# A graph layer's last 70 microseconds: output inside the condition, last squares on TensorE, residual loaded early

## The chip, the cores and the metric

The kernel runs on one core of one Trainium2 chip. Its time is device time in microseconds, the median of several executions. A core has a matrix engine (TensorE, PE in the profile, with its weight loads as PEld), three engines for elementwise work (VectorE or DVE, ScalarE or ACT, GpSimd or POOL) and a queue for transfers (SyncE, SP). Each engine works through its own list of instructions in order, and waits on semaphores for the others.

## The reference

One message-passing layer over 12,500 nodes and 412,500 edges, 96 features, float32. Edges are sorted by destination.

```
def _mlp(h, W, b, gamma, beta):
    h = relu(h @ W + b)
    mu, var = mean(h, axis=0), mean((h - mu)**2, axis=0)
    return gamma * (h - mu) * rsqrt(var + EPS) + beta

node_feat = _mlp(x, W_node, ...)
edge_feat = _mlp(edge_attr, W_edge, ...)
message   = _mlp(concat([x[src], x[dst], edge_feat]), W_msg, ...)
out       = layernorm(x + segment_sum(message, dst) + node_feat)
```

The normalization inside `_mlp` is over all rows, so the messages' statistics (the mean and the mean square of each of the 96 features over all edges) are complete only when the last edge has been worked on, and the output can start only then.

## The kernel before, in words

**Stages.** First the node tables `p_tab` and `q_tab` are computed (node features times two parts of `W_msg`) and written to memory; then the node part is computed, and x plus the node part, centred, is written to memory as `y0_d` (L257 to L287); then the edge part's statistics (L289 to L341); then comes the message loop (L379 to L630); then a condition (L785, L786); then the output (L790 to L827).

**Groups and blocks.** An edge tile has 128 edges. Four tiles are a group of 512 edges (806 groups), four groups are a block (202 blocks). For each tile GpSimd issues one indirect DMA (`gather`, L171) that fetches 128 rows of `p_tab`. GpSimd's whole list is these gathers, 3223 of them. The first 26 blocks are gathered before the loop and written to `spill` through two `stage` buffers; they are read back as `pb`. All other groups go into a ring of 26 buffers (`ring`, L93, tiles named `pg`). Each time the loop has used a group of the ring, the gather of the group 26 further on is issued (L619).

**The loop.** The order is written by hand (L566): for the loop, SP, GpSimd, TensorE, VectorE and ScalarE run their instructions in the order in which the program text issues them. For step `k`, `linear` (L475) computes the rest of the message on TensorE into `z`; `message` (L483) adds the gathered rows on VectorE and once a block builds `at`, a matrix of zeros and ones that says which edge belongs to which node; `first_part`, `second_part` and `third_part` (L502 to L530) apply the relu and split the result into three bf16 parts `h`; ScalarE also squares it into `sq`; `sums` (L532) multiplies `at` with `h` on TensorE, which sums the messages by node; `fold`, `turn` and `add` (L546 to L563) put the block's sums into `agg`, transposed by TensorE (`turn`), and the row of ones' sum into `total`. `moments` (L511) reduces `sq` over the tiles on VectorE and adds it to `squares`; after the loop one product with a column of ones sums `squares` over the partitions (L625). The last block has two groups, the last of them three tiles, so the last two steps are done singly.

**The condition.** The loop works only if every block's destinations lie within a window of nodes; `flag` says whether one does not. After the loop every engine loads the flag into a register (L785) and compares (L786). If the flag is set, `general` computes the same sums in another way, with long loops. With these inputs it isn't set, and each engine jumps over that code.

**The output.** Four products into an unused tile `busy` come first (L794). `norm` (L138) turns the statistics into a factor and an offset per feature; they are multiplied into a centring matrix `d` (L800, L802). Then come 13 groups of eight node blocks (the last has two): TensorE multiplies eight blocks of `agg` with `d` into `py` (three buffers), VectorE adds the residual `y0`, ScalarE squares, VectorE reduces over the features, ScalarE takes the root, VectorE the reciprocal, GpSimd multiplies, and SP's queue writes 384 KB out. The residual is loaded by ScalarE's queue into six buffers. Here the scheduler orders the instructions by itself.

Of the kernel before, what the change touches and what calls it, by code (L numbers as in the profile page):

```python
# [11 lines left out]
F32 = mybir.dt.float32  # L12
# [11 lines left out]
P = 128  # L24
# [17 lines left out]
NBK = 4  # L42
# [18 lines left out]
BUSY = 4  # L61
# [15 lines left out]
def gnn(ctx, tc, t):  # L77
# [13 lines left out]
    rpool, xpool = ExitStack(), ExitStack()  # L91
    nc.sync.dma_start(src_raw, t["src"][:, :RAW * BG * GT])
    ring = rpool.enter_context(tc.tile_pool(name="ring", bufs=RING))  # L93
# [86 lines left out]
    def blocks():  # L180

        for b in range(SPILL // BG):
            pg = ring.tile([P, BG, GT, C], F32, name="stage", bufs=2)
# [159 lines left out]
    def fast(ring):  # L343
        def ahead_of(g):
            return gather(g, ring.tile([P, GT, C], F32, name="pg"))

        with tc.manual_schedule(engines={ET.SP, ET.Pool}):
            nc.sync.dma_start(q_tab[:WM, :], zero[:WM])
            for r in range(WM + NN, WT, 64):
                n = min(64, WT - r)  # L350
                nc.sync.dma_start(q_tab[r:r + n, :], zero[:n])
            next(store)
            places()
            next(store)
            next(store)
            for i, _ in enumerate(nodes()):
                if i in (1, 5, 10):
                    next(store)
            xpool.close()
            n = 0  # L360
            for i, _ in enumerate(edge_norm()):
                if 73 * i >= 50 + 100 * n:
                    next(store, None)
                    n += 1
            for _ in store:
                pass
            got = {g: ahead_of(g) for g in range(SPILL, SPILL + RING)}
# [11 lines left out]
        with tc.tile_pool(name="fix", bufs=1) as fix, tc.tile_pool(name="msg", bufs=2) as work, \  # L379
# [63 lines left out]

            def convert(s):

                b = order[s]
                px = ps.tile([P, 2, GE], F32, name="pr", bufs=1)
                for i in range(BG):
                    for k in range(GT):
                        nc.tensor.transpose(px[:C, 0, k * P:(k + 1) * P], got[b * BG + i][:, k, :], ident)  # L450
                    xt = work.tile([C, GE], F32, name="xt", bufs=1)
                    nc.scalar.activation(xt, px[:C, 0, :], AF.Copy)
                    for k in range(GT):
                        nc.tensor.matmul(px[:, 1, k * C:(k + 1) * C], xt[:, k * P:(k + 1) * P], w_msg[:, 0, :],
                                         start=True, stop=True)
                    nc.vector.tensor_copy(got[b * BG + i], px[:, 1, :GT * C].rearrange("p (k c) -> p k c", c=C))
# [26 lines left out]
            def message(k):  # L483
# [5 lines left out]
                if i == min(2, NG - 1 - (g - i)):  # L489
# [64 lines left out]
            def add(s):  # L554

# [3 lines left out]
                    skip_runtime_bounds_check_because="they are nodes' numbers")  # L559
                pt = pas.pop(s)[:C + 1, GE - P:GE - P + NW]  # L560
                to = agg[:, bass.ds(val[0], NW - 1)]
                nc.vector.tensor_tensor(to, pt[:, :NW - 1], to, op=OP.add)
                nc.vector.tensor_add(total, pt[:, NW - 1:], total)  # L563

            n, ahead = len(steps), SPILL + RING
            with tc.manual_schedule(engines={ET.SP, ET.Pool, ET.PE, ET.DVE, ET.Activation}):  # L566
                load(0)
# [10 lines left out]
                for k in range(len(order) * BG + LATER + BG):  # L578
                    s, g = steps[min(k, n - 1)]
                    if k < n and g % BG == 0:  # L580
# [3 lines left out]
                    if k < n:  # L584
                        message(k)
                    j = k - LATER - BG - 1
                    if k < n and (k % 2 or k >= last):
                        whole, m = k < last, min(GT, NT - g * GT)
                        part = (k - 1,) if whole else (k, 1, m)
                        now = first_part(*part)  # L590
                        if waiting:
                            moments(*waiting)
                        waiting = now if whole else None
                        second_part(*part)
                    if j >= 0 and j % BG == 0:
                        fold(j // BG)
                    if j >= 2 and j % BG == 2:
                        add(j // BG)
                    if k < n and (k % 2 or k >= last):
                        third_part(*part)  # L600
                        if not whole:
                            moments(*now, min(P, E - (g * GT + m - 1) * P))
                    if j >= 1 and j % BG == 1:
                        turn(j // BG)
                    if 0 <= k - LATER < n:
                        sums(k - LATER)
                    if k < n and g % BG != 3 and s + 1 < len(order):
# [4 lines left out]
                    if k < n and g % BG == 3:  # L612
# [6 lines left out]
                    if k < n and g >= SPILL and ahead < NG:  # L619
# [4 lines left out]
            pq = ps.tile([P, GE], F32, name="pa")  # L624
            nc.tensor.matmul(pq[:C, :1], squares, ones, start=True, stop=True)  # L625
            nc.vector.tensor_scalar(s[:, 0:1], pq[:C, :1], 1.0 / E, None, op0=OP.mult)
# [3 lines left out]
            nc.vector.tensor_scalar(mstat[:, 1:2], s[:, 2:3], 0.0, None, op0=OP.max)  # L630

    def general():

        with tc.tile_pool(name="gd", bufs=1, space=DRAM) as gd, tc.tile_pool(name="gfix", bufs=1) as fix, \
# [31 lines left out]
            def gather(idx_s, idx_d, c, nt, rows):  # L666
                pg = work.tile([P, GT, C], F32, name="pg", bufs=4)
                qg = work.tile([P, GT, C], F32, name="qg", bufs=4)
# [7 lines left out]
            def message(n, gathered, ea, dstf, to_spare, c, nt, rows, stat):  # L676
# [13 lines left out]
                same = work.tile([P, GT, P], F32, name="same", bufs=3)  # L690
# [25 lines left out]
                sums = work.tile([P, GT, W], F32, name="sums", bufs=3)  # L716
# [25 lines left out]
            AHEAD = 2  # L742
            with tc.For_i(0, NI, 1) as it:
# [3 lines left out]
                for g in range(-AHEAD, IG):  # L747
# [4 lines left out]
                    ea = work.tile([EK, GE], F32, name="gea", bufs=3)  # L752
# [9 lines left out]
            for j, (t0, nt, rows) in enumerate(REST):  # L762
# [4 lines left out]
                ea = work.tile([EK, GE], F32, name="gea", bufs=3)  # L767
# [15 lines left out]
    fast(ring)  # L783
    rpool.close()
    bad = nc.values_load(flag, min_val=0, max_val=1, skip_runtime_bounds_check_because="a comparison's result")  # L785
    with tc.If(bad):  # L786
        general()


    with tc.tile_pool(name="fin", bufs=2) as work, tc.tile_pool(name="fin_ps", bufs=2, space=PSUM) as ps:  # L790

        busy = ps.tile([P, GE], F32, name="busy", bufs=1)
        for i in range(BUSY):
            nc.tensor.matmul(busy, ident, rel[:, i * P:(i + 1) * P, :].rearrange("p g t -> p (g t)"), start=True, stop=True)  # L794
        a_m, c_m = norm(mstat, v["g_msg"], v["beta_msg"], "msg")
        l = const.tile([C, C + 1], F32, name="l")
        nc.vector.tensor_scalar(l[:, :C], ident[:C, :C], a_m, None, op0=OP.mult)
        nc.vector.tensor_copy(l[:, C:C + 1], c_m)
        pd = ps.tile([C + 1, C], F32, name="pd", bufs=1)
        nc.tensor.matmul(pd, l, center, start=True, stop=True)  # L800
        d = const.tile([C + 1, C], F32, name="dm")
        nc.vector.tensor_copy(d, pd)  # L802

        out = t["out"]
        for i in range(0, NB, NBY):
            n = min(NBY, NB - i)
            y0 = work.tile([P, NBY, C], F32, name="y0", bufs=6)
            nc.scalar.dma_start(y0[:, :n, :], y0_d[i // NBY][:, :n * C].rearrange("p (b f) -> p b f", f=C))
            py = ps.tile([P, 2, GE], F32, name="py", bufs=3)
            for g in range(n):  # L810
                nc.tensor.matmul(py[:, g // NBK, g % NBK * C:(g % NBK + 1) * C],  # L811
                                 agg[:, WM + (i + g) * P:WM + (i + g + 1) * P], d, start=True, stop=True)
            sq = work.tile([P, NBY, C], F32, name="sq")
            sd = work.tile([P, NBY], F32, name="sd", bufs=3)
            y = work.tile([P, NBY, C], F32, name="y", bufs=3)
            if n == NBY:
                x = y0.rearrange("p (k b) f -> p k (b f)", k=2)
                nc.vector.tensor_add(x, py[:, :, :NBK * C], x)  # L818
            else:
                x = y0[:, :n, :].rearrange("p b f -> p (b f)")  # L820
                nc.vector.tensor_add(x, py[:, 0, :n * C], x)
            nc.scalar.activation(sq[:, :n, :], y0[:, :n, :], AF.Square)
            nc.vector.tensor_reduce(sd[:, :n], sq[:, :n, :], axis=AX.X, op=OP.add)  # L823
            nc.scalar.activation(sd[:, :n], sd[:, :n], AF.Sqrt, bias=eps, scale=1.0 / C)  # L824
            nc.vector.reciprocal(sd[:, :n], sd[:, :n])  # L825
            nc.gpsimd.tensor_tensor(y[:, :n, :], y0[:, :n, :], sd[:, :n].unsqueeze(2).to_broadcast([P, n, C]), op=OP.mult)  # L826
            nc.sync.dma_start(out.rearrange("(b p) f -> p b f", p=P)[:, i:i + n, :], y[:, :n, :])  # L827
# [34 lines left out]
```

## Time and profile before

| | us |
|---|---|
| median of 3 runs | 4117.61 (4116.02 to 4118.02) |
| the profiled execution | 4122.05 |
| its span, first to last instruction | 4120.3 |

| engine | busy us | share |
|---|---|---|
| TensorE, products | 3150.0 | 76% |
| TensorE, weight loads | 2259.1 | 55% |
| VectorE | 2576.7 | 63% |
| ScalarE | 2020.8 | 49% |
| GpSimd | 3067.8 | 74% |

Mean granted TensorE clock: 0.629 of full speed.

A row of the timeline reads: start, length, engine, line, operation, what it writes and reads, the number of instructions merged into the row, and in brackets the idle time of the engine before it with what ended it. A row of the stretches reads: from and to, its length, busy time of the engine asked for with the number of its instructions, the granted clock, the share of the DMA engines that was busy, and GB/s. Products in f32 appear as two records each. Starts of neighbouring instructions on one engine can overlap a little.

### The profile page before, as it was taken

The numbers are of one execution on the slowest core, as the hardware profiler recorded it, in microseconds if no ns is written. First come the engines' busy times: TensorE is split into PE (matmuls) and PEld (weight loads), VectorE is DVE, ScalarE is ACT, GpSimd is POOL, SyncE is SP. The second block draws the span as 40 slices with busy tenths as digits, with TensorE's granted clock in tenths as the row PEclk, the third lists the DMA queues.
The fourth block names the chain that finished last, engine by engine and source line by source line (L and its number), as shares of the span: only waits on it lengthen the run. The fifth ranks groups of instructions, "written<-read, shape, count | busy, mean of one in ns | idle before, by whom it ended". The sixth has DMA issues, their size and how long they took to land. (4 is left out here: it accounts for less than half of the span.)

```text
span 4120.3 us, 42684 instructions
## 1 busy us (share of the span) xinstructions
PE 3150.0 (76%) x13498; PEld 2259.1 (55%) x13498; DVE 2576.7 (63%) x4038; ACT 2020.8 (49%) x2418; POOL 3067.8 (74%) x3244
## 2 busy tenths in 40 slices
PE   4699967888878777777777677877777777777776
PEld 4465535666655555555555555555555555555554
DVE  2599994667766655665566556655666566655665
ACT  1287754556644444544444444544454454444443
POOL 6777777777777777777777777777777777777774
PEclk7655556667665656666666666666666666656666
DMA  8555532222222222222222222222222222222224
GB/s 244 168 117 107 106 78 57 54 54 56 56 54 46 54 52 55 52 48 53 53 48 53 53 55 53 46 54 54 54 46 54 53 54 46 54 53 55 46 53 112
DMA packets 190368, 274.07 MB, mean 67 GB/s; under 512 B 121571, under 2 KB 121956, under 8 KB 189126
## 3 DMA queue, kind: packets, MB, share of 16 engines
q0 software_dynamic: 103136, 158.62, 19.4%
q1 hardware_dynamic: 71684, 99.14, 8.7%
q10 hardware_dynamic: 15312, 13.47, 1.2%
q8 instruction: 111, 1.82, 0.2%
q14 instruction: 125, 1.02, 0.1%
HBM read 227.55 MB, written 43.43 MB: 66 GB/s over the span
## 5 line engine op out<-in xcount | busy, mean ns | idle before, releaser
L175 POOL DMA_INDIRECT pg<-p_tab,src x2807 | 2649.5, 944 | 856.1 <-issue 692.1
L479 PEld LDWEIGHTS z<-rhs,left 128*128 128x128 f32 x6446 | 1291.4, 295 | 1033.1 <-DVE h L530 909.0
L479 PE MATMUL z<-rhs,left 128*128 128x96 f32 x6446 | 1381.7, 386 | 588.5 <-DVE h L530 587.0
L542 PE MATMUL pa<-h,at 128*80 128x291 bf16 x3223 | 837.8, 406 | 191.1 <-DVE at L492 185.0
L505 ACT ACTIVATE h<-z 128x768 bf16<-128x768 f32 x404 | 330.1, 817 | 1324.0 <-DVE z L488 1315.9
L488 DVE TENSOR_TENSOR z<-z,pg 128x384 f32<-128x384 f32 x702 | 395.0, 563 | 783.1 <-DMA pg<-p_tab,src 771.5
L542 PEld LDWEIGHTS <-at 128*80 128x80 bf16 x3223 | 496.1, 167 | 300.9 <-DVE at L492 228.4
L515 DVE TENSOR_REDUCE sum_of<-sq 128x96 f32<-128x768 f32 x404 | 591.9, 1465 | 0.0
L473 ACT ACTIVATE left<-pr 127x1024 f32<-127x1024 f32 x403 | 411.0, 1020 | 347.5 <-PE pr L465 346.9
L530 DVE TENSOR_TENSOR h<-z,h 128x768 bf16<-128x768 f32 x404 | 387.0, 958 | 244.2 <-ACT h L525 244.1
L465 PE MATMUL pr<-ea,we 7*127 7x512 f32 x1404 | 512.3, 813 | 17.3 <-DMA ea<-rel_d 12.5
L175 POOL DMA_INDIRECT stage<-p_tab,src x368 | 353.9, 962 | 128.3 <-issue 106.8
L524 DVE SCALAR_TENSOR_TENSOR z<-z,h 128x768 f32<-128x768 f32 x404 | 387.3, 959 | 28.2 <-ACT sq L507 28.1
L306 PE MATMUL pr<-ea,wide 10*128 10x512 f32 x1212 | 371.3, 1061 | 21.2 <-DMA ea<-in_ea 21.2
L312 DVE BATCH_NORM_STATS2 estats<-r 128x6 f32<-128x512 f32 x606 | 361.2, 676 | 27.6 <-ACT r L310 27.6
L310 ACT ACTIVATE r<-pr 128x1024 f32<-128x1024 f32 x303 | 292.9, 1024 | 143.6 <-PE pr L306 116.9
L525 ACT ACTIVATE h<-z 128x768 bf16<-128x768 f32 x404 | 329.2, 815 | 66.7 <-DVE z L524 66.7
L508 ACT ACTIVATE sq<-sq 128x768 f32<-128x768 f32 x404 | 339.7, 841 | 13.1
L507 ACT ACTIVATE sq<-z 128x768 f32<-128x768 f32 x404 | 322.9, 799 | 0.0
L306 PEld LDWEIGHTS pr<-ea,wide 10*128 10x128 f32 x1212 | 208.2, 319 | 182.9 <-issue 81.0
L492 DVE TENSOR_TENSOR at<-rel,z 128x496 bf16<-128x496 f32 x202 | 135.6, 671 | 262.3 <-PE z L479 262.0
L465 PEld LDWEIGHTS pr<-ea,we 7*127 7x127 f32 x1404 | 135.0, 236 | 139.4 <-issue 108.6
(127 smaller groups left out, 1145.2 us busy)
## 6 DMA issues: line engine op xcount, KB each, us to landing
pg<-p_tab,src POOLq DMA_INDIRECT x2807
spill<-stage SPq DMA_DIRECT2D x26, 768.0 KB
pb<-spill SPq DMA_DIRECT2D x26, 768.0 KB
ea<-in_ea SPq DMA_DIRECT2D x75, 160.0 KB
rhs<-q_tab SPq DMA_DIRECT2D x202, 46.5 KB
ea<-in_ea SPq DMA_DIRECT2D x352, 20.0 KB
stage<-p_tab,src POOLq DMA_INDIRECT x368
y_d<-y0s SPq DMA_DIRECT2D x12, 384.0 KB
```

What stands on the lines that cost most here:

```text
L175: nc.gpsimd.indirect_dma_start(out=pg[:, i, :], out_offset=None, in_=tab[:, :], in_offset=bass.IndirectOffsetOnAxis(ap=idx[:, k:k + 1], ax ...
L306: nc.tensor.matmul(pr[:, k % 2, :], wide[Q * i:Q * i + 2 * EK, :], ea[Q * i:Q * i + 2 * EK, b % J, :], start=True, stop=True)
L312: nc.vector.bn_stats(stats[:, (k - o) % NS, (k - o) // NS, :], r[:, 1 - o, :])
L465: nc.tensor.matmul(prs[s, half][:C + WN, i, :], we[o:o + EK + 2, :], block[s][o:o + EK + 2, :], start=True, stop=True)
L473: nc.scalar.activation(x[:C + WN, 2 * half:2 * half + n, :], pr[:C + WN, :n, :], AF.Relu)
L479: nc.tensor.matmul(zb[k // 2 % 2][:, k % 2, i * C:(i + 1) * C], left[s % 2][:KR, g % BG, i * P:(i + 1) * P], rhs[:KR, s % RB, g % BG, :], ...
L488: nc.vector.tensor_add(z, z, got.pop(g)[:, :n, :])
L508: nc.scalar.activation(sq[:, :m, :n, :], sq[:, :m, :n, :], AF.Square)
L515: nc.vector.tensor_reduce(sum_of, sq[:, :m, :whole, :].rearrange("p g t c -> p c g t"), axis=AX.XY, op=OP.add)
L524: nc.vector.scalar_tensor_tensor(z, z, 0.0, h[0], op0=OP.max, op1=OP.subtract)
L530: nc.vector.tensor_tensor(h[2], z, h[1], op=OP.subtract)
L542: nc.tensor.matmul(pas[s][:NW, :3 * (C + 1)], at[s % HB][:r, i, o + NW * t:o + NW * (t + 1)], h[:r, t, :, :].rearrange("p a c -> p (a c)") ...
```

## The change

- **Ring and stage.** The ring has 13 buffers of two groups for 26 of one. The `stage` buffers have a pool of their own, closed before the loop.
- **Residual.** Where the ring has no further group to gather, the pairs that come free take the 13 pieces of `y0_d`, loaded by SP's queue, each when both groups of the pair have been used.
- **The flag** is loaded into registers ahead of the loop, on every engine, so on GpSimd between two gathers.
- **The last two steps** are written out. The last `moments` of VectorE are gone: `columns` multiplies each tile's squares with a column of ones on TensorE and accumulates in PSUM (one product for `squares`, 8, 4, 2 and 1 for the last tiles). `at` of the last block is built one group earlier. `add` takes `total` first.
- **The output** is a function that stands in both arms of the condition; the arm that these inputs take follows the comparison directly, and it ends with a jump over the other arm. The `busy` products are gone. In the last but one group ScalarE scales, in eight instructions, and in the last VectorE; GpSimd does the other eleven.
- In the arm that is not taken, `general` has fewer buffers.

```diff
-    ring = rpool.enter_context(tc.tile_pool(name="ring", bufs=RING))
+    ring = rpool.enter_context(tc.tile_pool(name="ring", bufs=RING // 2))
+    stage = spool.enter_context(tc.tile_pool(name="stage", bufs=2))
...
     def fast(ring):
+        y0s, pair = [], [None]
+
         def ahead_of(g):
-            return gather(g, ring.tile([P, GT, C], F32, name="pg"))
+            if g % 2 == 0:
+                pair[0] = ring.tile([P, 2, GT, C], F32, name="pg")
+            if g < NG:
+                return gather(g, pair[0][:, g % 2, :, :])
+            i = (g - NG) // 2
+            if g % 2 == 0 and i * NBY < NB:
+                y0s.append(pair[0].rearrange("p g t c -> p (g t c)"))
+                m = min(NBY, NB - i * NBY) * C
+                nc.sync.dma_start(y0s[i][:, :m], y0_d[i][:, :m])
...
+            def columns(to, x):
+                for i in range(x.shape[1]):
+                    nc.tensor.matmul(to, x[:, i, :], ones, start=False, stop=False)
...
-                if i == min(2, NG - 1 - (g - i)):
+                if i == (2 if g - i + BG <= NG else 0):
...
+                nc.vector.tensor_add(total, pt[:, NW - 1:], total)
                 nc.vector.tensor_tensor(to, pt[:, :NW - 1], to, op=OP.add)
-                nc.vector.tensor_add(total, pt[:, NW - 1:], total)
...
             with tc.manual_schedule(engines={ET.SP, ET.Pool, ET.PE, ET.DVE, ET.Activation}):
+                bad = nc.values_load(flag, min_val=0, max_val=1, skip_runtime_bounds_check_because="a comparison's result")
...
+                s, g = len(order) - 1, steps[last][1]
+                m, r = NT - (g + 1) * GT, E - (NT - 1) * P
+                message(last)
+                sq = first_part(last, 1, GT)[0]
+                turn(s - 2)
+                sums(last - 2)
+                sums(last - 1)
+                square_sum = ps.tile([P, 2, GE], F32, name="pr", bufs=1)[:C, 0, :1]
+                nc.tensor.matmul(square_sum, squares, ones, start=True, stop=False)
+                for i in range(2):
+                    columns(square_sum, waiting[0][:, i, :, :])
+                add(s - 2, place(s - 2))
+                second_part(last, 1, GT)
+                third_part(last, 1, GT)
+                ahead_of(ahead)
+                message(n - 1)
+                sq_end = first_part(n - 1, 1, m)[0]
+                fold(s - 1)
+                turn(s - 1)
+                sums(last)
+                columns(square_sum, sq[:, 0, :, :])
+                second_part(n - 1, 1, m)
+                third_part(n - 1, 1, m)
+                sums(n - 1)
+                columns(square_sum, sq_end[:, 0, :m - 1, :])
+                nc.tensor.matmul(square_sum, sq_end[:r, 0, m - 1, :], ones[:r], start=False, stop=True)
+                add(s - 1, place(s - 1))
+                at_end = place(s)
+                fold(s)
+                turn(s)
+                add(s, at_end)
+                ahead_of(ahead + 1)
...
+    y0s, bad = fast(ring)
+    with tc.If(bad, preferred_fallthrough_block=False) as cmp:
+        general()
+        output(y0s, "gen")
+    with cmp.Else():
+        output(y0s, "win")
     rpool.close()
-    bad = nc.values_load(flag, min_val=0, max_val=1, skip_runtime_bounds_check_because="a comparison's result")
-    with tc.If(bad):
-        general()
...
-        busy = ps.tile([P, GE], F32, name="busy", bufs=1)
-        for i in range(BUSY):
-            nc.tensor.matmul(busy, ident, rel[:, i * P:(i + 1) * P, :].rearrange("p g t -> p (g t)"), start=True, stop=True)
...
-            y0 = work.tile([P, NBY, C], F32, name="y0", bufs=6)
-            nc.scalar.dma_start(y0[:, :n, :], y0_d[i // NBY][:, :n * C].rearrange("p (b f) -> p b f", f=C))
...
-            nc.gpsimd.tensor_tensor(y[:, :n, :], y0[:, :n, :], sd[:, :n].unsqueeze(2).to_broadcast([P, n, C]), op=OP.mult)
...
+                if i == last - 1:
+                    for g in range(n):
+                        nc.scalar.activation(y[:, g, :], y[:, g, :], AF.Copy, scale=sd[:, g:g + 1])
+                else:
+                    (nc.vector if i == last else nc.gpsimd).tensor_tensor(y[:, :n, :], y[:, :n, :], by, op=OP.mult)
```

More of the change, by code (lines that the diff above doesn't have):

```diff
@@ L60 @@
 CL, CE = 2, 2
-BUSY = 4
 J = 8
@@ L182, in blocks @@
         for b in range(SPILL // BG):
-            pg = ring.tile([P, BG, GT, C], F32, name="stage", bufs=2)
+            pg = stage.tile([P, BG, GT, C], F32, name="stage")
             for i in range(BG):
@@ L577, in fast @@
                 waiting, last = None, BG * (len(order) - 1)
-                for k in range(len(order) * BG + LATER + BG):
-                    s, g = steps[min(k, n - 1)]
-                    if k < n and g % BG == 0:
+                for k in range(last):
+                    s, g = steps[k]
+                    if g % BG == 0:
                         if s + 2 < len(order):
@@ L583, in fast @@
                             fetch(s + 2)
-                    if k < n:
-                        message(k)
+                    message(k)
                     j = k - LATER - BG - 1
[L587 to L590, printed above, removed]
+                    if k % 2:
+                        now = first_part(k - 1)
                         if waiting:
                             moments(*waiting)
-                        waiting = now if whole else None
-                        second_part(*part)
+                        waiting = now
+                        second_part(k - 1)
                     if j >= 0 and j % BG == 0:
@@ L597, in fast @@
                     if j >= 2 and j % BG == 2:
[L598 to L602, printed above, removed]
+                        add(j // BG, place(j // BG))
+                    if k % 2:
+                        third_part(k - 1)
                     if j >= 1 and j % BG == 1:
                         turn(j // BG)
-                    if 0 <= k - LATER < n:
+                    if k >= LATER:
                         sums(k - LATER)
-                    if k < n and g % BG != 3 and s + 1 < len(order):
+                    if g % BG != 3 and s + 1 < len(order):
                         if g % 2:
@@ L618, in fast @@
                         linear(k + 3)
[L619 removed]
+                    if g >= SPILL:
                         got[ahead] = ahead_of(ahead)
                         ahead += 1
+                s, g = len(order) - 1, steps[last][1]
[30 more added lines that the diff above has]
+                ahead_of(ahead + 1)
             s = fix.tile([C, 3], F32, name="s")
[L624 to L626 removed]
+            nc.vector.tensor_scalar(s[:, 0:1], square_sum, 1.0 / E, None, op0=OP.mult)
             nc.vector.tensor_scalar(mstat[:, 0:1], total[:C], 1.0 / E, None, op0=OP.mult)
@@ L689, in message @@
                                         ident[:rows, :rows])
-                same = work.tile([P, GT, P], F32, name="same", bufs=3)
+                same = work.tile([P, GT, P], F32, name="same", bufs=2)
                 nc.vector.tensor_tensor(
```

86 lines of the change are left out of this document (45 added, 41 removed).

## The prediction

> **What bounds the kernel now.** I read the page's groups first, then GpSimd's waits, then the timeline of the last 70 us, then the stretches with their granted clock.
>
> ```profile
> span 4120.3 us, 42684 instructions
> ...
> L175 POOL DMA_INDIRECT pg<-p_tab,src x2807 | 2649.5, 944 | 856.1 <-issue 692.1
> ```
> ```profile
> POOL pg L175 <- issue: 692.1, 2271, 0.3
> ...
> POOL pg L175 <- DMA pg<-p_tab,src: 69.2, 225, 0.9
> ...
> POOL pg L175 <- DVE total L563: 26.5, 87, 0.3
> ```
>
> A gather takes 0.94 us and is followed by 0.30 us of idle, whatever the releaser named: the longest idle time behind VectorE is 0.3 us. So GpSimd issues one gather each 1.25 us without a stop from the first `pg` to the last, and the ring is never full. All that is added on GpSimd's queue counts in full; what the other engines do before the last gather counts for nothing. The rest of the time is the tail:
>
> ```profile
> 4051.64 0.94 POOL L175 DMA_INDIRECT pg<-p_tab,src  x1 [0.30 <-issue]
> ...
> 4055.80 0.57 DVE L488 TENSOR_TENSOR z<-z,pg 128x384 f32<-128x384 f32 x1 [3.67 <-DMA pg<-p_tab,src]
> ...
> 4060.40 0.94 POOL L175 DMA_INDIRECT pg<-p_tab,src  x1 [0.30 <-issue]
> 4060.73 0.56 DVE L488 TENSOR_TENSOR z<-z,pg 128x384 f32<-128x384 f32 x1
> 4060.87 2.11 PE L542 MATMUL pa<-h,at 128*80 128x291 bf16 x8 [1.03 <-DVE h L530]
> ...
> 4065.47 0.46 DVE L488 TENSOR_TENSOR z<-z,pg 128x288 f32<-128x288 f32 x1
> 4065.96 0.42 DVE L492 TENSOR_TENSOR at<-rel,z 128x248 bf16<-128x248 f32 x1
> ...
> 4068.02 1.93 PE L542 MATMUL pa<-h,at 128*80 128x291 bf16 x7 [5.05 <-DVE total L563]
> 4068.10 0.46 DVE L530 TENSOR_TENSOR h<-z,h 128x288 bf16<-128x288 f32 x1
> ...
> 4071.08 0.43 PE L552 MATMUL pa<-ident,by_node 80*97 80x80 f32 x1
> ...
> 4072.45 0.15 DVE L630 TENSOR_SCALAR mstat<-s 96x1 f32<-96x1 f32 x1
> 4075.75 0.29 ACT L141 ACTIVATE norm_msg<-mstat,eps 96x1 f32<-96x1 f32 x1 [7.68 <-DVEq L786]
> ...
> 4075.86 6.24 PE L794 MATMUL busy<-rel,ident 128*128 128x512 f32 x8 [4.35 <-DVEq L786]
> ...
> 4076.90 0.15 DVE L798 COPY l<-norm_msg 96x1 f32<-96x1 f32 x1
> ...
> 4082.31 0.26 DVE L802 COPY dm<-pd 97x96 f32<-97x96 f32 x1 [5.26 <-PE pd L800]
> 4082.62 21.63 PEld L811 LDWEIGHTS py<-dm,agg 97*128 97x128 f32 x192 [0.51 <-DVE dm L802]
> 4082.62 21.79 PE L811 MATMUL py<-dm,agg 97*128 97x96 f32 x192 [0.35 <-DVE dm L802]
> 4084.74 0.96 DVE L818 TENSOR_TENSOR y<-py,y 128x768 f32<-128x768 f32 x1 [2.17 <-DMA y<-y_d]
> ...
> 4113.06 0.17 DVE L825 RECIPROCAL sd<-sd 128x2 f32<-128x2 f32 x1 [0.36 <-ACT sd L824]
> 4113.81 2.06 POOL L826 TENSOR_TENSOR y<-y,sd 128x768 f32<-128x768 f32 x2 [0.20 <-POOL y L826]
> ```
>
> Read: a gather lands 4.16 us after it starts (4051.64 to 4055.80). The statistics stand at 4072.60; all engines pass the condition's load and jump, and ScalarE starts the norm 3.15 us later; `l` is ready at 4077.05, but TensorE works on the eight `busy` records until 4082.10; the output products start at 4082.62 and the output takes 37.7 us from there.
>
> **The clock.** This decides the case.
>
> ```profile
> 166.08 28.48 PE L278 MATMUL py<-center,xp 96*128 96x96 f32 x132 [7.74 <-DVE y0s L282]
> ```
> ```profile
> 166.00:168.00 2.00, 1.92 (x9) 0.50 0.57 206
> ...
> 192.00:194.00 2.00, 2.00 (x11) 0.50 0.99 392
> ```
> ```profile
> 4080.00:4081.00 1.00, 1.00 (x2) 0.50 0.86 252
> 4081.00:4082.00 1.00, 1.00 (x4) 0.98 0.90 249
> ...
> 4103.00:4104.00 1.00, 1.00 (x11) 1.00 1.16 327
> ```
>
> The column behind TensorE's busy time is the granted clock. The `busy` products (128 rows, 512 columns) raise it from 0.50 to 1.00 at 4081.0, 5.1 us after they start, and the output runs on at 1.00: 21.79 us for 192 records, 0.113 us each. The nodes' products of L278 have nearly the output's form (96 rows for 97, 96 columns moving, f32), ran without a pause for 28.48 us and stayed at 0.50 in every stretch: 0.214 to 0.216 us each. Without `busy`, the output starts at 0.50, and the nearest row says that it stays there.
>
> **Part by part.** (1) Ring of pairs, `stage` in its own pool: each second gather now waits for a group one later; with no idle time over 0.3 us behind VectorE that is nothing, and the cover is a ring of 26 groups (130 us of issue). (2) The flag is loaded before the loop, on GpSimd's queue as well, between two gathers. No row has that load. On VectorE the load of `base` lies hidden:
>
> ```profile
> 3966.49 0.96 DVE L524 SCALAR_TENSOR_TENSOR z<-z,h 128x768 f32<-128x768 f32 x1
> ...
> 3967.36 0.23 DVE L562 TENSOR_TENSOR agg<-pa,agg 97x79 f32 x1
> ```
>
> It takes at most 0.87 us of sequencer time; bounds 0 to 0.9, taken 0.6, since GpSimd shows no overlap between instructions. (3) Residual loads move from ScalarE's queue into the last 130 us on SP's, 13 of them, each waiting for the pair's last message; `load` of the next blocks stands behind on SP, but its rows are wanted a block (20 us) later. Against the gathers in flight they could cost the landing of the next to last group a microsecond or two, which (4) hides. In the output they take away the waits behind `y<-y_d`, the first 2.17 us.
>
> (4) Last squares on TensorE. VectorE loses reductions and adds between 4060.7 and 4069.4; the last message can start when its gather lands, 4060.40 + 4.16 = 4064.56 for 4065.47, and `at` is built a group earlier: its `h` is ready at 4064.56 + (4068.56 - 4065.47 - 0.42) = 4067.2. But TensorE gets 16 products of one column, two records each, in its strict order.
>
> ```profile
> 607.18 1.09 PE L330 MATMUL pr<-part,pick 128*96 128x2 f32 x6 [20.17 <-DVE part L319]
> ...
> 4009.87 1.86 PE L479 MATMUL z<-rhs,left 128*128 128x96 f32 x8
> ```
>
> Nearest is L330 (same weights, two columns, clock 0.50): six records with their end in 1.09 us, some 0.16 us each; the other end is the 0.232 us of a record with 96 columns. At 0.16: nine products end at 4062.98 + 2.8 = 4065.8, the turn and four sums take 1.2 (4067.0), four products 1.3 (4068.3), the last three sums 0.9 (4069.2), three products 1.0 (4070.2); the last turn, issued as the last of these drain, starts near 4069.8, and from its start to the statistics it is 1.5 us (4071.08 to 4072.60): they stand at some 4071.3, 1.3 us gained. At 0.232 it is 2.3 us later, a loss of 1.
>
> (5) Near arm: the norm starts 0.1 us behind the statistics for 3.15: 4071.4. `l` takes 1.30 us as before (4075.75 to 4077.05): 4072.7. The centring product and `dm` take 1.2 at half clock (0.5 between 4082.10 and 4082.62): 4073.9, with the flag's 0.6 4074.5. `busy` (L794) no longer holds TensorE. So the output starts 8.1 us earlier. The jump over the other arm now stands at the arm's end; its 2 to 3 us run beside the last transfer, and I add 0.3 (0 to 2.5).
>
> (6) Output. At 0.50: 196 records by 0.214 us are 41.9 us, for the 22 of before; TensorE then bounds the stage, since VectorE needs some 2 us for eight blocks (0.96 + 0.90 + 0.17) and TensorE 3.4.
>
> ```profile
> 4066.41 0.41 ACT L505 ACTIVATE h<-z 128x288 bf16<-128x288 f32 x1 [2.45 <-DVE at L492]
> 4066.72 0.40 ACT L507 ACTIVATE sq<-z 128x288 f32<-128x288 f32 x1
> ...
> 4105.29 0.90 DVE L823 TENSOR_REDUCE sd<-sq 128x8 f32<-128x768 f32 x1
> ...
> 4110.44 0.35 DVE L821 TENSOR_TENSOR y<-py,y 128x192 f32<-128x192 f32 x1
> ...
> 4110.87 0.36 ACT L822 ACTIVATE sq<-y 128x192 f32<-128x192 f32 x1
> ```
>
> Behind the last full products (41.3): add 0.96, square 0.84, reduction 0.90, root and reciprocal with the small group's add 0.6, eight scalings on ScalarE at about 0.22 each 1.9 (estimated from 0.41 us durations 0.31 apart for 288 columns), the small group's root, reciprocal and product 0.9: 47.4 us. From the last product to the end of the span stand 4120.3 - 4115.87 = 4.4 us, and the jump's 0.3: 52.1 us.
>
> **Sum.** 4074.5 + 52.1 = 4126.6 for a span of 4120.3, 6.3 us longer: 8.1 gained ahead of the output, 14.4 lost in it. The profiled execution took 4122.05 us with 1.75 around its span; the median of the three runs is 4117.61, 4.4 below. I carry the difference over: 4117.6 + 6.3 = 4123.9.
>
> **Rivals.** A: the output's products raise the clock themselves. For it: they have 97 rows, which may count otherwise than 96, and z products with sums do raise it within the loop; against it, L278. With the clock doubled 5 us in, the second group is ready at 6.2 us, VectorE's remaining work (11 full groups' adds, 12 reductions and reciprocals, the small add: 23.7 us at those durations) ends at 29.9, scalings and last group 3.0, the end 4.7: 37.6. 4074.5 + 37.6 = 4112.1, 8.2 less, and with the first groups a little earlier 9: 4108.6 to 4109.4, taken 4109. [...]
>
> B, slower: the one-column products go at the 96-column pace, so TensorE's tail is 2.3 us later: 4126.2. It decides from about 0.22 us a record, with the clock at 0.50. Against it: L330.
>
> C: the near arm is no near arm, that is, the condition still jumps for 3 us: 4127. Against it: in the program's list the arm's instructions follow the comparison directly.
>
> **How the numbers follow.** 0.2% (8.2 us) is about what a measurement of this kernel can tell: 4109.4 and 4125.8 are the bounds. Forecast 58%: 4123.9, own range 4120.5 (flag 0, pace of the columns faster, clock late) to 4126.5 (flag 0.9, the jump 2.5 exposed): 47 of it within, 11 above. A 30%: half below 4109.4, as the clock's moment is free by some 3 us: 15 faster, 15 the same. B 5%, C 4%, both slower. 3% for what I don't see, split between faster and slower. Faster 0.17, same 0.62, slower 0.21. The range takes in A and B: 4107.5 to 4127.
>
> **What would show it.** The granted clock in the output: 0.50 throughout and records 0.214 us apart, output products about 42 us long, VectorE idle behind TensorE in each group. Last gather within 1 us of 4060.4; the norm's root directly behind the statistics, near 4071.5; first output product near 4074.5. The prediction is wrong if the clock rises within the first 7 us of the output, if GpSimd waits on the ring, or if the statistics stand later than 4073.

## The result, and the profile after

The changed kernel takes 4125.66 us (median of 20 runs, 4121.88 to 4128.66) against 4118.42 us (20 runs, 4115.37 to 4121.41) for the kernel before: ratio 1.0017, 95% interval 1.0010 to 1.0024. It is 7.2 us slower, about as forecast (4123.9), and within the 0.2% that the forecast called no change. The profiled execution took 4124.84 us.

The page of the changed kernel and its timeline from the last gather on:

```profile
span 4123.1 us, 42434 instructions
...
L175 POOL DMA_INDIRECT pg<-p_tab,src x2807 | 2649.5, 944 | 855.8 <-issue 800.3
```
```profile
4056.36 0.94 POOL L175 DMA_INDIRECT pg<-p_tab,src  x1 [0.30 <-issue]
...
4059.10 2.70 PE L457 MATMUL pr<-ones,sq 128*96 128x1 f32 x16
...
4060.56 0.47 DVE L503 TENSOR_TENSOR z<-z,pg 128x288 f32<-128x288 f32 x1
...
4065.64 0.43 PE L567 MATMUL pa<-ident,by_node 80*97 80x80 f32 x1
...
4066.96 0.15 DVE L675 TENSOR_SCALAR mstat<-s 96x1 f32<-96x1 f32 x1
4067.20 0.29 ACT L141 ACTIVATE norm_win<-mstat,eps 96x1 f32<-96x1 f32 x1 [4.01 <-DVE mstat L675]
...
4069.68 42.13 PE L848 MATMUL py<-dm,agg 97*128 97x96 f32 x196 [0.35 <-DVE dm L840]
...
4114.64 2.23 ACT L863 ACTIVATE y<-y,sd 128x96 f32<-128x96 f32 x8
...
4117.28 0.36 DVE L865 TENSOR_TENSOR y<-y,sd 128x192 f32<-128x192 f32 x1
```

The last gather starts at 4056.36 here and at 4060.40 before; that lead arises in the first 550 us, while the `stage` gathers run, and it has the size of the scatter of the two profiles (before 3.6 us above its median of 20 runs, after 0.8 below); whether the `stage` buffers' own pool has a part in it was not tested. So both are read from the last gather on. Before, 59.9 us lie between its start and the end of the span; now it is 66.7. The statistics stand 10.75 us behind it (4067.11) for 12.2. The first output product starts 13.3 us behind it for 22.2. The output itself takes 53.4 us (4069.68 to 4123.1) for 37.7. So 8.9 us are gained ahead of the output and 15.7 lost in it.

Stretches of ten microseconds within the output of the changed kernel (TensorE's busy time with its instructions, granted clock, DMA share, GB/s), and what VectorE waited for there:

```profile
4070.00:4080.00 10.00, 10.00 (x48) 0.50 0.00 0
...
4100.00:4110.00 10.00, 10.00 (x49) 0.50 0.44 120
```
```profile
DVE y L854 <- PE py L848: 19.6, 12, 3.8
```

TensorE never stops and the clock never leaves 0.50. Before, VectorE mostly set the pace (it waited 5.2 us for the residual and 1.4 for TensorE), and the last four records of the output's products came only after a wait for it:

```profile
4105.32 0.69 PE L811 MATMUL py<-dm,agg 97*128 97x96 f32 x4 [0.90 <-DVE y L818]
```

Now VectorE waits for TensorE in twelve groups of thirteen.

### The profile page after: what moved, and what is told of

It is laid out like the page before. It is cut to its first block, busy times and chain, and to the rows that moved or that the text cites. A ratio compares the mean times of both kernels' runs of the same rounds, so it can differ in the third digit from the quotient of the medians.

```text
span 4123.1 us, 42434 instructions
## 1 busy us (share of the span) xinstructions
PE 3165.9 (77%) x13520; PEld 2284.9 (55%) x13520; DVE 2576.4 (62%) x4032; ACT 2020.8 (49%) x2426; POOL 3065.2 (74%) x3242
## 4 chain that ended last, share of the span: by engine, by line
POOL 47%; issue 22%; DMA 13%; PE 9%; DVE 7%; ACT 1%; SPq 0%; DVEq 0%; POOLq 0%; ACTq 0%
POOL pg L175 42%; DMA pg<-p_tab,src 9%; POOL stage L175 6%; PE z L494 3%; DMA stage<-p_tab,src 3%; DVE sum_of L530 2%; PE pa L557 2%; PE pr L480 1%; DVE z L503 1%; DVE z L539 1%; PE py L848 1%; ACT h L540 1%; PE pr L469 1%; DMA w_node<-in_L_gnn_W_node 1%; DMA q_tab<-trow 0%
## 5 line engine op out<-in xcount | busy, mean ns | idle before, releaser
L557 PE MATMUL pa<-h,at 128*80 128x291 bf16 x3223 | 846.7, 409 | 184.0 <-DVE at L507 182.9
L480 PE MATMUL pr<-ea,we 7*127 7x512 f32 x1404 | 497.6, 791 | 17.1 <-DMA ea<-rel_d 12.6
```

The source lines that it names most:

```text
L480: nc.tensor.matmul(prs[s, half][:C + WN, i, :], we[o:o + EK + 2, :], block[s][o:o + EK + 2, :], start=True, stop=True)
L557: nc.tensor.matmul(pas[s][:NW, :3 * (C + 1)], at[s % HB][:r, i, o + NW * t:o + NW * (t + 1)], h[:r, t, :, :].rearrange("p a c -> p (a c)") ...
```

## The experiments

They ran on three other chips, and there the part ahead of the output is slower: the kernel before takes 5557 to 5563 us. In a run of the changed kernel the span is 1397 us longer than on the first chip, 356 of them ahead of the loop's first message and 1041 in the loop. The gathers don't set the pace; GpSimd waits for the ring. The waits (total, times, longest) show it in a run of the changed kernel, below the largest wait of all in that run, and in a run of the kernel before without its unread products:

```profile
ACT left L488 <- remote: 1939.8, 154, 23.2
...
POOL pg L175 <- DVE z L503: 1145.6, 175, 108.6
```
```profile
POOL pg L175 <- DVE z L488: 1149.0, 175, 107.7
```

So the ring is full there with either kernel. ScalarE and VectorE pause within the loop for something that the trace does not name (it says only `remote`; VectorE waits 221.7 us for it ahead of `at` in the thousand from 2500 to 3500 of that run of the changed kernel), and the time of one kernel varies by up to 50 us between executions. The changed kernel stood at 1.0028 (interval 1.0012 to 1.0044) of the kernel before on one of these chips and at 0.9948 (0.9927 to 0.9968) on another; that difference lies ahead of the last statistics and its cause stays open. So the runs are read from the stretch that the change is about, from the start of the last instruction on the statistics (`mstat`) to the end of the span. It does not depend on the chip: the changed kernel has 56.14, 56.19 and 56.13 us in three profiles on three chips; the kernel before has 47.85. Medians are compared only within one chip.

| run | first product behind the statistics | products | statistics to the end |
|---|---|---|---|
| kernel before | 10.17 | 21.79 (192 of 196 records; the last four follow a wait) | 47.85 |
| changed kernel | 2.72 | 42.13 | 56.14 |
| before without the unread products | 5.75 | 42.13 | 58.06 |
| changed, unread products back | 5.43 | 22.12 | 41.43 |
| changed, 112 rows | 2.72 | 42.13 | 56.13 |
| changed, 120 rows | 2.72 | 42.13 | 56.09 |
| changed, 128 rows | 2.72 | 24.20 | 40.84 |
| 128 rows, two unread products | 3.29 | 22.13 | 39.33 |
| 128 rows, GpSimd scales twelve groups | 2.71 | 23.99 | 41.15 |
| changed, arms exchanged | 5.01 | 42.13 | 56.81 |
| changed, squares on VectorE | 2.71 | 42.13 | 56.13 |

**The unread products, back in the changed kernel.**

```diff
+            busy = ps.tile([P, GE], F32, name="busy", bufs=1)
+            for i in range(4):
+                nc.tensor.matmul(busy, ident, rel[:, i * P:(i + 1) * P, :].rearrange("p g t -> p (g t)"), start=True, stop=True)
             a_m, c_m = norm(mstat, v["g_msg"], v["beta_msg"], name)
```


> The changed kernel with the four unread products back, at the head of the output. Theory (the clock): they start near 10.5 us behind the start of the last gather, raise the granted clock to 1.00 some 5 us later and end at about 17; the output products start near 17.5 for 13.3 now, take about 22 us for 42, VectorE bounds the stage, and the end comes 53 to 55 us behind the last gather for 66.7: 11 to 15 us less than the changed kernel, so some 4111 us. Rival (the late jump, ScalarE's eight scalings or the residual's new place hold the output, and the clock alone doesn't): a gain below 6 us, with VectorE idle for something else than TensorE.

Timeline and stretches of this run:

```profile
5478.58 5.99 PE L835 MATMUL busy<-rel,ident 128*128 128x512 f32 x8
...
5479.67 0.15 DVE L675 TENSOR_SCALAR mstat<-s 96x1 f32<-96x1 f32 x1
...
5485.10 22.12 PE L851 MATMUL py<-dm,agg 97*128 97x96 f32 x196 [0.35 <-DVE dm L843]
```
```profile
5482.00:5484.00 2.00, 2.00 (x5) 0.67 0.00 0
5484.00:5486.00 2.00, 1.65 (x12) 1.00 0.00 0
```

The clock rises some 4.7 us behind the start of the unread products and the output runs at 1.00: 41.43 us for 56.14, 14.7 us less, within what the theory gave. The late jump, the scalings and the residual's place are all still there, so none of them is what makes the output slow. Against the kernel before the stretch is 6.4 us shorter: with the unread products kept, the same change would by these profiles have been a gain (no run of it exists on the first chip). On its own chip this version takes 5519.15 us, 0.9922 of before (0.9899 to 0.9944); the changed kernel itself was not timed there.

**The unread products, out of the kernel before.** Its lines with `busy` are deleted, nothing else.

> The kernel before without its four unread products, nothing else. Theory (the clock): the output products start some 4 us earlier, at 17.9 us behind the last gather for 22.2, but at clock 0.50, 0.214 us a record, 42 us for 22; the output takes some 51 us for 37.7: about 9 us slower than before, some 4127 us. Rival (the output raises the clock by itself there, and the changed kernel's slow output has another cause): about 4 us faster than before.

```profile
5495.24 0.15 DVE L630 TENSOR_SCALAR mstat<-s 96x1 f32<-96x1 f32 x1
5498.58 0.29 ACT L141 ACTIVATE norm_msg<-mstat,eps 96x1 f32<-96x1 f32 x1 [7.72 <-DVEq L786]
...
5500.99 42.13 PE L808 MATMUL py<-dm,agg 97*128 97x96 f32 x196 [0.35 <-DVE dm L799]
```

The products start 4.4 us earlier than before and take 42.13 us; from the statistics to the end it is 10.2 us more than before, and the time is 1.0024 of before (1.0006 to 1.0042), 13 us, where 9 were expected. This one edit alone costs more in that stretch than the whole change, which costs 8.3. The two runs together show that the slow output is the unread products' absence.

**What holds the clock down: 128, 120 and 112 rows.** The products read 97 rows of `agg` and `dm`. Padded with zero rows they read more, and the result is the same. The question is whether the rows decide.

```diff
-    agg = const.tile([C + 1, WT], F32, name="agg")
+    agg = const.tile([P, WT], F32, name="agg")
+    d = const.tile([P, C], F32, name="dm")
+    nc.vector.memset(d, 0.0)
...
-                to = agg[:, bass.ds(val, NW - 1)]
+                to = agg[:C + 1, bass.ds(val, NW - 1)]
...
-            d = work.tile([C + 1, C], F32, name="dm", bufs=1)
-            nc.vector.tensor_copy(d, pd)
+            nc.vector.tensor_copy(d[:C + 1], pd)
```


> The changed kernel with the output's products over 128 rows for 97: the table of sums and the centring matrix get 31 more rows, all zero, so the result is the same. [...] Rival (rows don't count; the short moving side of 96 columns is what keeps the clock down): clock 0.50 to the end, within 1 us of the changed kernel.

```profile
5469.96 0.15 DVE L677 TENSOR_SCALAR mstat<-s 96x1 f32<-96x1 f32 x1
...
5472.68 24.20 PE L849 MATMUL py<-dm,agg 128*128 128x96 f32 x196 [0.35 <-DVE dm L841]
```
```profile
5474.00:5476.00 2.00, 2.00 (x12) 0.50 0.00 0
5476.00:5478.00 2.00, 2.00 (x15) 0.73 0.00 0
5478.00:5480.00 2.00, 2.00 (x21) 1.00 0.00 0
```

With 128 rows the same products raise the clock by themselves, some 4.4 us behind the first. Then 112 and 120 rows (`P` replaced by that number in the two tiles):

> The changed kernel with 112 rows in the output's products, 15 of them zero. If what counts is rows times busy time against a threshold that lies between 97 and 128, this halves the gap. Theory 1 (threshold below 112): the clock rises, perhaps later than with 128 rows (3.9 us), and the products take 24 to 32 us. Theory 2 (only full or nearly full arrays count): 0.50 throughout, 42 us.

> The changed kernel with 120 rows in the output's products, 23 of them zero; 112 rows left the clock at 0.50, 128 raised it. If the bound is a share of the array's rows below 120: products of 24 to 30 us. If it is between 120 and 128: 42 us, clock 0.50.

Timelines of 112 rows, then of 120, with a stretch of the latter:

```profile
5537.49 42.13 PE L849 MATMUL py<-dm,agg 112*128 112x96 f32 x196 [0.35 <-DVE dm L841]
```
```profile
5467.73 42.13 PE L849 MATMUL py<-dm,agg 120*128 120x96 f32 x196 [0.35 <-DVE dm L841]
```
```profile
5498.00:5508.00 10.00, 10.00 (x49) 0.50 0.44 120
```

Neither raises it. All four products have the same columns and type, and the same pace at the start (VectorE's first addition, behind sixteen records, starts 3.76 us after the first product with 97 rows, 3.77 with 120 and with 128), so in these runs it is the rows, and the bound lies above 120. Products of another type or with other columns were not tried. The 128-row version was then timed beside the changed kernel on one chip:

> The changed kernel as it is, once more as the yardstick of the two beside it: 56.1 to 56.2 us from the statistics to the end of the span, as in both profiles so far.

> The changed kernel with 128 rows in the output's products, again, beside the changed kernel on one chip. Theory (rows decide the clock): 40.8 us from the statistics to the end of the span, as in its first profile, and its median 15 us below the changed kernel's. Rival (the 15 us of the profiles don't carry over to the time, for the ring or the transfers give some back): less than 10 us below it.

The changed kernel takes 5532.24 us there (7 runs, 5517.36 to 5545.73), with 128 rows 5508.22 (6 runs, 5503.53 to 5516.13), the kernel before 5561.48; with 128 rows it is 0.9900 of before (0.9881 to 0.9919), for the changed kernel's 0.9948. The medians differ by 24.0 us, where the theory had 15; the profiles of these two differ by 56.13 - 40.59 = 15.5 us behind the statistics. The other 8 us lie ahead of them, where one kernel scatters by more than that, and they are no gain of this edit that the runs show. No run of it exists on the first chip; by the stretch it would be near 4125.66 - 15.3 = 4110 us there (an estimate).

**128 rows, and two unread products.**

```diff
+            for i in range(2):
+                nc.tensor.matmul(busy, ident, rel[:, i * P:(i + 1) * P, :].rearrange("p g t -> p (g t)"), start=True, stop=True)
```


> 128 rows, and two of the four unread products back at the head of the output: they fill TensorE's idle time before the centring product and hold it up by less than 0.5 us. [...]

```profile
5460.78 3.70 PE L837 MATMUL busy<-rel,ident 128*128 128x512 f32 x4
...
5461.87 0.15 DVE L677 TENSOR_SCALAR mstat<-s 96x1 f32<-96x1 f32 x1
...
5465.16 22.13 PE L852 MATMUL py<-dm,agg 128*128 128x96 f32 x196 [0.35 <-DVE dm L844]
```
```profile
5464.00:5465.00 1.00, 0.81 (x3) 0.50 0.00 0
5465.00:5466.00 1.00, 0.84 (x7) 1.00 0.00 0
```

The clock rises at 5465.0, 4.2 us behind the first unread product, in the idle time just ahead of the output, and no output product runs at 0.50. The products start 0.57 us later (up to 0.5 was expected), and the stretch is 39.33 us, 1.3 to 1.5 less than with 128 rows alone. That is too little for the times: 5519.47 us (5502.94 to 5535.40), against 5508.22, is inconclusive.

**GpSimd scales all twelve full groups**, with 128 rows.

```diff
-                if i == last - 1:
-                    for g in range(n):
-                        nc.scalar.activation(y[:, g, :], y[:, g, :], AF.Copy, scale=sd[:, g:g + 1])
-                else:
-                    (nc.vector if i == last else nc.gpsimd).tensor_tensor(y[:, :n, :], y[:, :n, :], by, op=OP.mult)
+                (nc.vector if i == last else nc.gpsimd).tensor_tensor(y[:, :n, :], y[:, :n, :], by, op=OP.mult)
```


> The changed kernel with 128 rows in the output's products, and GpSimd scaling all twelve full groups (ScalarE's eight scalings of the last but one gone). [...] Rival (the scalings on ScalarE are what keeps the end short, since GpSimd is late): 41 us or more, no better than with 128 rows alone (40.8).

Timeline of its end, and a stretch behind it (VectorE's busy time, clock, DMA share, GB/s):

```profile
5558.30 1.47 POOL L863 TENSOR_TENSOR y<-y,sd 128x768 f32<-128x768 f32 x1 [0.49 <-POOL y L863]
...
5559.34 0.64 DVE L863 TENSOR_TENSOR y<-y,sd 128x192 f32<-128x192 f32 x1
```
```profile
5561.00:5562.00 1.00, 0.00 (x0) 0.50 1.02 257
```

The last multiplication ends 31.1 us behind the first product, for 32.6 with ScalarE's scalings. But the span ends 7.3 us behind it for 5.5. Of these 1.8 us, 0.5 are transfers: those of the last groups fill all DMA engines at 257 GB/s, one behind the other, until some 2.7 us behind the last multiplication, for 2.1. The other 1.3 lie behind the transfers, some 4.6 us for 3.4 to the end of the span, and their cause is open. The stretch is 41.15 us, no better; the rival's number came true, while the late GpSimd that it gave as the reason does not show. Beside it on one chip the changed kernel takes 5582.29 us and this one 5567.53, 14.8 less; the profiles show 15.0 behind the statistics.

> The changed kernel as it is, as the yardstick for the others beside it. Every theory: the clock is 0.50 through the whole output, 196 records in 42.1 us, and from the statistics to the end of the span 56.1 us, as in its first profile; its time against the kernel before is the first chip's, 1.0017, unless this chip's loop is limited otherwise.

It came so behind the statistics, with 42.13 us of products and 56.19 us to the end; its ratio to the kernel before is the 1.0028 given above.

**The arms exchanged**, so that the taken arm is reached by a jump (`preferred_fallthrough_block=True`).

> The changed kernel with its two arms exchanged: the arm that is taken now stands behind the other, and is reached by a jump. Theory: the norm starts 3.1 us behind the statistics for 0.09, and the 1 us between the last product and the end of the span goes, since no jump is left at the end: about 2 us slower than the changed kernel, some 4127.5. Rival (what stands before the norm is the flag's load, which is still ahead of the loop, not the jump): the norm starts less than 1 us behind the statistics, and the time is the same or 1 us less.

```profile
5480.89 0.15 DVE L675 TENSOR_SCALAR mstat<-s 96x1 f32<-96x1 f32 x1
5481.14 0.29 ACT L141 ACTIVATE norm_win<-mstat,eps 96x1 f32<-96x1 f32 x1 [4.02 <-DVE mstat L675]
5483.82 0.16 DVE L142 RECIPROCAL norm_win<-norm_win 96x1 f32<-96x1 f32 x1 [2.78 <-issue]
...
5485.90 42.13 PE L848 MATMUL py<-dm,agg 97*128 97x96 f32 x196 [0.35 <-DVE dm L840]
...
5533.80 0.36 DVE L865 TENSOR_TENSOR y<-y,sd 128x192 f32<-128x192 f32 x1
```

ScalarE starts the root 0.1 us behind the statistics, as the rival had it; but VectorE, which works until then, stands idle for 2.8 us before the next step, as the theory had it: ScalarE's jump lay in its idle time, VectorE's does not. From the statistics to the first product it is 5.01 us: 5.75 with the flag's load and the jump behind the statistics (the kernel before without its unread products), 5.01 with the jump alone, 2.72 with neither. So the jump is worth 2.3 us and the load some 0.7 (an estimate, since the 5.75 is of a kernel that differs in more). At the end, 3.5 us lie behind the last multiplication for 5.5 in the changed kernel. In sum 0.67 us more than the changed kernel, where the theory expected 2 and the rival none or a gain: the near arm moves most of the jump's cost to the end.

The DMA queue that the profile names `instruction`, in the last 13 us of the changed kernel, and in the last 11 us of this one (packets, MB, share):

```profile
q14 instruction: 8, 0.07, 1.4%
```
```profile
q14 instruction: 1, 0.01, 0.2%
```

The late jump goes with eight packets of that queue, five of them in the last 5 us of the span; the kernel before has one in its last 13 us. Whether the engines wait for these packets no trace shows.

**The last squares on VectorE again.** `moments` is called in the last two steps as before, the one-column products are gone, and one product with the column of ones stands at the end.

```diff
-                for i in range(2):
-                    columns(square_sum, waiting[0][:, i, :, :])
+                moments(*waiting)
...
-                columns(square_sum, sq[:, 0, :, :])
+                moments(sq, 1, GT)
...
-                columns(square_sum, sq_end[:, 0, :m - 1, :])
-                nc.tensor.matmul(square_sum, sq_end[:r, 0, m - 1, :], ones[:r], start=False, stop=True)
+                moments(sq_end, 1, m, r)
```


> The changed kernel with the last steps' squares summed on VectorE again, as before, and one product with the column of ones at the end; all else stays. Theory (the squares on TensorE bring what the traces differ by, 1.45 us between the last gather and the statistics, because VectorE's reductions delayed the last message): the last message is some 0.9 to 1.5 us later behind its predecessor, and from the last but one message to the statistics it is 1 to 2 us longer than in the changed kernel. Rival (the gain came from building the comparison matrix a group earlier and from the order of the last additions, which stay here): within 0.4 us of the changed kernel.

Timeline of the changed kernel on this chip, then of the variant:

```profile
5512.78 0.56 DVE L503 TENSOR_TENSOR z<-z,pg 128x384 f32<-128x384 f32 x1
...
5516.51 0.47 DVE L503 TENSOR_TENSOR z<-z,pg 128x288 f32<-128x288 f32 x1
...
5522.91 0.15 DVE L675 TENSOR_SCALAR mstat<-s 96x1 f32<-96x1 f32 x1
```
```profile
5528.72 0.56 DVE L503 TENSOR_TENSOR z<-z,pg 128x384 f32<-128x384 f32 x1
...
5534.44 0.46 DVE L503 TENSOR_TENSOR z<-z,pg 128x288 f32<-128x288 f32 x1
...
5540.57 0.15 DVE L673 TENSOR_SCALAR mstat<-s 96x1 f32<-96x1 f32 x1
```

From the last but one message to the statistics it is 11.85 us for 10.13: 1.7 us for the squares, as the theory had it (medians: 5588.89 us for 5582.29, within the loop's scatter); the last message is 2.0 us later behind its predecessor, more than expected. On the first chip the same stretch is 10.13 us for 11.72 before, 1.6; from the last gather on it is 1.45, because the last but one message stands 0.47 us behind that gather for 0.33. The parts of the change that the variant keeps, the matrix a group earlier and the order of the last additions, gave nothing by themselves: 11.85 us with them, 11.72 before.

## Why the prediction was right, point by point

(1) *Ring of pairs: nothing.* Right on the first chip: GpSimd's longest wait behind VectorE within `pg` stays 0.3 us, and its longest of all, on a transfer ahead of the loop, is 0.6 for 0.9. On chips where the ring is full it was not tested.

(2) *The flag's load: 0.6 of 0 to 0.9.* Too much. The gathers of the loop stay at 0.94 us with 0.30 behind each; the load cost nothing that the trace shows. Behind the statistics it was worth some 0.7 us.

(3) *Residual loads on SP: nothing.* Right. In the output VectorE's first wait is for TensorE (3.82 us), and the last message starts 4.2 us behind its gather, about the 4.16 that the prediction read for a landing.

(4) *Last squares on TensorE: 1.3 us.* Right in size: 1.45, and the experiment gives the squares 1.7. Sixteen records took 2.70 us, 0.17 each for 0.16, so rival B falls. One premise was met by luck: the working let the last message start when its gather lands. It starts 3.73 us behind its predecessor, directly behind VectorE's own work, and it does so too in a run on another chip, where that gather started 94 us ahead of the message; so VectorE's list holds it, and the landing only falls on the same moment.

(5) *Near arm: the norm 0.1 us behind the statistics.* Right, so rival C falls; output start 8.1 us earlier, measured 8.9, and most of that difference is the flag's 0.6. The jump at the arm's end was the mis-sized term: 0.3 was taken of 0 to 2.5. From the last multiplication to the end of the span it is 5.5 us for 4.4, and 3.5 without that jump, so it costs 1 us against before and 1.9 against the other order of the arms. My argument that it runs beside the last transfer was wrong: the transfers end 2.2 us behind the last multiplication (2.1 with the arms exchanged), and the span ends 3.3 us behind them (1.5).

(6) *Output at clock 0.50: 52.1 us.* Right in kind, 53.4 in size. Products 42.13 us (41.9), clock 0.50 throughout; 0.6 us more lie between the last full products and the last multiplication (eight scalings took 2.23 us for 1.9, and the last group's root waits behind them), and 0.8 in the jump above.

Ahead of the output the working was 0.8 us too slow, in it 1.3 too fast; the sum, 6.3 us longer, was 6.8 from the last gather and 7.2 in the medians. The two errors have opposite signs, so part of that agreement is luck.

The marks in absolute time were missed: the last gather starts at 4056.36, where 4060.4 within 1 us was named, and the norm and the first product stand earlier than named by about as much. That is the lead of the first 550 us, which the working did not foresee.

Rival A, the largest, did not come. The row that decided against it, the nodes' products of 96 rows at 0.50 for 28.48 us, was the right one to read, though the forecast could not say why: 97 rows and 96 behave alike, 128 do not; the z products, which with the sums raise it in the loop (0.50 from 1000 to 1002 us of the kernel before, 1.00 from 1004 to 1006), have 128 rows as well. In the runs products of 128 rows raised the clock 3.9 to 5.2 us behind their start: the unread ones after 5.2 us in the kernel before, 4.7 in the changed kernel and 4.2 as two ahead of 128 rows, the output's own with 128 rows after 4.4 and, where GpSimd scales all twelve groups, 3.9. Products of 97, 112 or 120 rows kept TensorE busy for 42 us at 0.50. That the clock's moment is free by some 3 us, by which the forecast split rival A's chance, no run shows; those five times lie within 1.3 us.

## What to carry to other kernels

Before deleting work whose result nobody reads, look at the granted clock before and behind it: here four such products of 6 us were worth 14 to 15 us of the next stage. Where a stage of f32 products with fewer than 128 rows stays at clock 0.50, try padding the rows with zeros (shown here for 97 rows and 96 columns): the products cost the same at the start and went from 42 to 24 us in all, and the stretch behind the statistics is then 40.8 us, 7 less than before the change. A jump that is moved behind the last work is still paid: here 1.9 of its 2.3 us.

## What the runs showed of the hardware that I had not expected

- In these runs the granted clock depends on the rows that f32 products of 96 columns use: 97, 112 and 120 rows stay at 0.50 for 42 us without a pause, 128 rows, 31 of them zeros, go to 1.00 after 3.9 to 4.4 us.
- Two unread products ahead of the stage, 3.7 us in all, are enough: the clock rises 4.2 us behind the first of them and the output runs at 1.00 (196 records in 22.13 us), although the centring product of 96 rows and 0.35 us of idle time lie between.
- The taken jump cost an engine that arrives late 2.3 us, and one that waits there nothing: ScalarE and VectorE took the same jump, and only VectorE's showed (2.78 us of idle time for 0.49).
- The kernel before takes 4118 us on one chip and about 5560 on three others, where the engines pause for something that the trace does not name, while the changed kernel's last 56 us are alike to 0.1 us on three chips.
